# Four graph layers on one core: the heads' second scores go to every row by way of DRAM, and every kind of operation gets its own shift in the order

## The chip, the core and the metric

The kernel runs on one core of one Trainium2 chip. A core has five engines that each work through their own list of instructions: TensorE (matrix products; the profile calls it PE, and its weight loads PEld), VectorE (DVE), ScalarE (ACT), GpSimd (POOL) and SyncE (SP), which here only issues DMAs. An engine takes its instructions strictly in the order of its list, so an instruction that waits holds up all that stand behind it. The metric is the time of one execution on the device in microseconds (us); smaller is better.

## The reference, cut to what matters

The input `x` holds 128 graphs of 64 nodes with 512 features, in float32. All graphs share one 64 x 64 adjacency `adj`. Four layers follow each other, each `x = layernorm(x + layer(x))`. The first multiplies by `W` and aggregates over `adj`. The second is a graph attention with 4 heads, an output attention and a feed-forward part. The third and fourth are single-head attentions. The change lies in the attention of the four heads:

```python
Wh = jnp.einsum('bnf,hfo->bhno', x, W)
f1 = jnp.einsum('bhno,ho->bhn', Wh, a[:, :O])
f2 = jnp.einsum('bhno,ho->bhn', Wh, a[:, O:])
e = f1[:, :, :, None] + f2[:, :, None, :]
e = jnp.where(e > 0, e, LEAKY_ALPHA * e)
e = jnp.where(adj[None, None] > 0, e, NEG_INF)
attn = jax.nn.softmax(e, axis=-1)
```

For every head and graph, `e[n, m]` is a first score of node n plus a second score of node m. On the chip node n is a row (a partition), so the second scores, which lie one to a row, have to be brought into every row, along the free dimension. How they get there is what changes.

## The kernel before

The 8192 rows of `x` (128 graphs x 64 nodes) are cut into 32 pairs (`p`) of two tiles (`t`) of 128 rows. One tile holds two graphs. A pair goes through stages, each a Python generator: `stage_first` (layer one), `stage_scores` (scores and attention weights of the four heads, and the aggregated rows `ys`), `stage_heads` (the products of the heads with `W_heads`), `stage_project` (the product with `W_out`), `stage_out` (output attention, feed-forward part, norms), and `stage_gat` twice (layers three and four). The last pair has its own stages for the tail. The large products are done with seven half-size products in place of eight (`seven`, `strassen`), and the right-hand parts for them stream in from DRAM all the time (`ws_...`, from copies `d_...` that the kernel wrote there at its start). About five pairs are under way at once, each in another stage.

Nothing is issued while the stages run. `Plan.note` records each operation as a `Step` with a rank (its number, minus 1000 inside `nc.soon()`). Then `Plan.order` goes through all steps as a list scheduler would. It keeps a clock for each of the five engines, takes durations from the table `cost`, adds `WAIT` plus a `SLACK` between engines, hands out the buffers of the pools (`NEAR` says how far ahead of its turn a step may take one), and whenever an engine is free it takes the ready step of the lowest rank. `Plan.play` issues the steps in the order that comes out. All instructions are therefore issued from one line, L314, and the profile tells them apart only by the names of their tiles.

The heads' attention of a pair is `attention_heads`. `f` is a 128 x 2 x 8 tile: for each row the first and the second score of 4 heads in 2 tiles (8 columns each). For pairs 0 and 1 `f` comes from products on PE (`fp`), for the other 30 from dot products on VectorE (`dots`, tiles `j`), against score rows that are broadcast from DRAM (`rows<-d_h`). The spreading of the second scores before the change:

- VectorE multiplies the 8 second scores with `ident2`, two 64 x 64 identities on top of each other, into `dg`, 128 x 512 (8 blocks of 64 columns, each a diagonal);
- PE multiplies `dg` with `bones`, a 128 x 128 matrix with two 64 x 64 blocks of ones, into the PSUM tile `bc`: row n of `bc` then holds the second scores of all 64 nodes of its own graph, for 8 heads and tiles;
- VectorE adds the first score to it (`e`), and goes on with leaky relu, mask, maximum, subtraction, ScalarE's exp, sum, reciprocal and a last product, back into `e`;
- PE transposes `e` (`pt`), ScalarE copies the result to `aT`, and PE multiplies it with `x` (`yp`), the input of `stage_heads`.

The other attentions of the kernel spread their scores with transposes of a broadcast column (`attention`; also called `bc`, with `ident` and `f` as inputs) and are not changed.

Of the kernel before, what the change touches and what calls it, by code (L numbers as in the profile page):

```python
# [12 lines left out]
FP = mybir.dt.float32  # L13
# [3 lines left out]
ALU = mybir.AluOpType  # L17
# [3 lines left out]
P = 128  # L21
# [4 lines left out]
ts = lambda i, n: slice(i * n, (i + 1) * n)  # L26
# [11 lines left out]

WAIT = 0.2
NEAR = 160
SLACK = {"tensor": 0.8, "sync": 0.4}


class Slots:


    def __init__(self, n):
        self.free, self.queue = [(0.0, i, None) for i in range(n)], []  # L50
        self.openers = []
# [26 lines left out]
class View:  # L78
# [63 lines left out]
class Step:  # L142
    def __init__(self, engine, rank):
        self.engine, self.rank = engine, rank
        self.calls, self.after, self.behind, self.port = [], set(), set(), False
        self.opens, self.uses = [], set()
        self.takes, self.lands = 0.0, 0.0


class Plan:  # L150
# [23 lines left out]
    def note(self, engine, name, args, kw):  # L174
        if self.joined:
            s = self.joined[0]
            assert s.engine == engine
        else:
            s = Step(engine, len(self.steps) - self.early)
            self.steps.append(s)  # L180
            if self.joined is not None:
                self.joined.append(s)
        out = [kw[k] for k in ("out", "accum_out") if k in kw] + (
            [] if "out" in kw or not args else [args[0]]
        )
        views = [(v, True) for v in out if isinstance(v, View)] + [
            (v, False)
            for v in [*args, *kw.values()]
            if isinstance(v, View) and not any(v is o for o in out)
        ]  # L190
        for v, writes in views:
            t = v.tile
            writes = writes or t.pool.space is PSUM
            if not t.seen:
                s.opens.append(t)
            else:
                s.behind.add(t.seen[0][0])
            s.uses.add(t)
            s.after.update(o for o, r, w in t.seen if (w or writes) and v.meets(r))
            t.seen.append((s, v.region, writes))  # L200
        s.after.discard(s)
        s.behind -= {s} | s.after
        s.calls.append((name, args, kw))
        takes, s.lands = cost(engine, name, args, kw, out)
        if engine in ("vector", "gpsimd"):

            both = [v for v, writes in views if not writes and v.tile.pool.space is not PSUM]
            s.port = len(both) > 1 and (engine == "vector" or size_of(out) > 2)
        s.takes += takes

    def order(self):
# [21 lines left out]
        def late(s, e):  # L233
            return 0.0 if s.engine == e else WAIT + SLACK.get(s.engine, 0.3)

# [3 lines left out]
        def take(slots):  # L239

            while slots.queue:
                s = slots.queue[0][1]
                while slots in slots.openers[-1].given:
                    slots.openers.pop()
                if s.no > slots.openers[-1].no + NEAR:
                    return
# [62 lines left out]
    def play(self):  # L309
        real = lambda v: v.real() if isinstance(v, View) else v  # L310
        with self.tc.manual_schedule():
            for s in self.order():
                for name, args, kw in s.calls:
                    getattr(getattr(self.tc.nc, s.engine), name)(  # L314
                        *map(real, args), **{k: real(v) for k, v in kw.items()}
                    )
# [35 lines left out]
def gnn_stack_kernel(  # L352
# [24 lines left out]
    nc = Plan(tc)  # L377
    NT, D = x.shape
    N = adj.shape[0]
# [3 lines left out]
    G = T * H  # L383
# [56 lines left out]
    ident2 = cp.tile([P, N], FP, tag="ident2", name="ident2")  # L440
# [5 lines left out]
    never = cp.tile([P, 1], FP, tag="never", name="never")  # L446
# [12 lines left out]
    has = cp.tile([P, 1], FP, tag="has", name="has")  # L459
# [19 lines left out]
    aTg = [cp.tile([P, T, P], FP, tag=f"aTg{i}", name=f"aTg{i}") for i in range(2)]  # L479
# [44 lines left out]
    for h in range(H):  # L524
        w = wp.tile([P, KC // 2, 7, D // 2], FP, tag=f"wh{h}", name=f"wh{h}")
        for s in range(2):
            nc.sync.dma_start(
                out=w[:, :, 2 * s : 2 * s + 2, :].rearrange("p c h o -> p c (h o)"),
                in_=W_heads[h, ts(s, D // 2), :].rearrange("(c p) o -> p c o", p=P),
# [199 lines left out]
                    accum_out=f(s, t),  # L729
                )  # L730

    def attention_heads(f, name):

        bc3 = [P, G, N]

        dg = unit.tile([P, G, N], FP, tag="dg", name=f"dg_{name}")
        nc.vector.tensor_tensor(
            dg,
            f[:, 1, :].unsqueeze(2).to_broadcast(bc3),
            ident2.unsqueeze(1).to_broadcast(bc3),  # L740
            ALU.mult,
        )
        yield 2.0
        ps = psum.tile([P, G, N], FP, tag="b", name=f"bc_{name}")
        nc.tensor.matmul(ps, lhsT=bones, rhs=dg, start=True, stop=True)

        e = unit.tile([P, G, N], FP, tag="e", name=f"e_{name}")
        nc.vector.tensor_tensor(e, ps, f[:, 0, :].unsqueeze(2).to_broadcast(bc3), ALU.add)
        nc.vector.scalar_tensor_tensor(ps, e, 0.01, e, ALU.mult, ALU.max)
        nc.vector.copy_predicated(  # L750
            ps, mask1.unsqueeze(1).to_broadcast(bc3), fill1.unsqueeze(1).to_broadcast(bc3)
        )
        mx = small.tile([P, G], FP, tag="mx", name=f"mx_{name}")
        nc.vector.tensor_reduce(mx, ps, AX.X, ALU.max)
        nc.vector.tensor_tensor(ps, ps, mx.unsqueeze(2).to_broadcast(bc3), ALU.subtract)
        nc.scalar.activation(ps, ps, AF.Exp)
        sm = small.tile([P, G], FP, tag="sm", name=f"sm_{name}")
        nc.vector.tensor_reduce(sm, ps, AX.X, ALU.add)
        r = small.tile([P, G], FP, tag="r", name=f"r_{name}")
        nc.vector.reciprocal(r, sm)  # L760
        nc.vector.tensor_tensor(e, ps, r.unsqueeze(2).to_broadcast(bc3), ALU.mult)
        yield 10.0

        pt = psum.tile([P, G // 2, P], FP, tag="b", name=f"pt_{name}")
        with nc.together():
            for q in range(G // 2):
                nc.tensor.transpose(
                    pt[:, q, :], e[:, 2 * q : 2 * q + 2, :].rearrange("p s j -> p (s j)"), ident
                )
        aT = unit.tile([P, G // 2, 2, N], FP, tag="aTh", name=f"aT_{name}")  # L770
        for b in range(2):
            for s in range(2):
                nc.scalar.copy(aT[ts(b, N), :, s, :], pt[ts(s, N), :, ts(b, N)])
        return aT
# [64 lines left out]
    ys = {}  # L839
# [54 lines left out]
    def stage_scores(p):  # L894
# [4 lines left out]
        f = small.tile([P, 2, G], FP, tag="f", name=f"f_{p}")  # L899
        if p < 2:  # L900

            ps = psum.tile([P, T, 2, H], FP, tag="b", name=f"fp_{p}")
            for t in range(T):
# [14 lines left out]
        for h2 in range(H // 2 if p >= 2 else 0):  # L918
            for s in range(2):
                r = rows([score["h"][s * H + 2 * h2 + i, :] for i in range(2)], f"{p}_{h2}_{s}")  # L920
# [3 lines left out]
                    x, r, f"1_{p}_{h2}_{s}",  # L924
                )
        yield 3.0
        aT = yield from attention_heads(f, f"1_{p}")
        yield 3.0


        yh = []
        for q in range(H // 2):
            y = unit.tile([P, KC, 2, T, P], FP, tag="ys", bufs=2, name=f"ys_{p}_{q}")
            for t in range(T):
                ps = [
                    psum.tile([P, KC, 2, N], FP, tag="b", name=f"yp_{p}_{q}_{t}_{b}")
                    for b in range(2)
                ]
# [411 lines left out]
```

## Time and profile before

| what | value |
|---|---|
| median of three timed runs | 3346.63 us (3344.84 to 3348.06) |
| the profiled execution: its time, and its span from the first to the last instruction | 3347.62 us, 3345.8 us |
| PE, busy share of the span | 98% (3284.4 us) |
| PE weight loads | 86% |
| VectorE, ScalarE, GpSimd | 72%, 41%, 50% |
| DMA engines, mean busy share; moved | 64.9%; 718 MB |
| granted PE clock, mean | 0.993 |
| products `bc<-dg` (2 records each) | 64 records, 33.7 us busy |
| products `dg` on VectorE | 32, 22.5 us busy |

A PE record in this profile is longer than the spacing at which records follow each other, since they overlap in the pipeline; so what an operation costs on PE is read from the start of one group to the start of the next in the timeline. One float32 product shows as two records, a transpose as one.

### The profile page before, as it was taken

The page shows a single profiled execution, that of the slowest core. Times are in us where ns is not written, and L with a number is a line of the kernel's source. Part 1 is how long each engine was busy: PE and PEld are TensorE (multiplying, and loading weights), DVE is VectorE, ACT ScalarE, POOL GpSimd, SP SyncE. Part 2 cuts the span into 40 slices and gives each one's busy share as a digit, 9 for nine tenths or more (in the row PEclk, how much of TensorE's full clock was granted, in tenths as well). Part 3 has the DMA queues.
Part 4 walks back from the last instruction along what each step waited for, and adds up shares of the span by engine and source line. Part 5 has one row for each costly group of instructions (what it writes and reads, how often), then busy time and mean ns, then how long its engine had stood idle before and what let it go on. Part 6 is the DMA issues. An engine that isn't in the chain of part 4 may idle for free.

```text
span 3345.8 us, 59820 instructions
## 1 busy us (share of the span) xinstructions
PE 3284.4 (98%) x21298; PEld 2888.7 (86%) x21298; DVE 2420.4 (72%) x5698; ACT 1363.8 (41%) x3196; POOL 1684.7 (50%) x1860
## 2 busy tenths in 40 slices
PE   8999999999999999999999999999999999999997
PEld 4888888988988988989888989889889889888884
DVE  5477677777777777777777777777777777777756
ACT  2444344444444443443443443434444444444332
POOL 6745345554455554455554555544555544555442
PEclk9999999999999999999999999999999999999998
DMA  8956656667666666666666666676666666666752
GB/s 309 323 168 199 216 197 215 214 212 235 203 216 218 215 215 224 200 224 215 217 226 213 200 224 218 210 232 204 209 220 216 217 228 201 217 217 208 243 183 66
DMA packets 301062, 718.08 MB, mean 215 GB/s; under 512 B 32560, under 2 KB 41824, under 8 KB 300768
## 3 DMA queue, kind: packets, MB, share of 16 engines
q1 hardware_dynamic: 300768, 714.27, 64.9%
q8 instruction: 171, 2.80, 0.3%
q14 instruction: 123, 1.01, 0.1%
HBM read 680.82 MB, written 33.32 MB: 213 GB/s over the span
## 4 chain that ended last, share of the span: by engine, by line
PE 93%; DVE 2%; DMA 2%; POOL 2%; issue 1%; ACT 0%; SPq 0%; POOLq 0%; DVEq 0%
PE stx_h L314 13%; PE stx_o L314 13%; PE stx L314 12%; PE sty_h L314 10%; PE sty_o L314 10%; PE sty L314 9%; PE hidp L314 5%; PE yp L314 4%; PE gp L314 3%; PE stx_y L314 3%; PE sty_y L314 2%; PE axp L314 2%; PE bc L314 1%; DMA rows<-d_h 1%; PE op L314 1%; PE l L314 1%
## 5 line engine op out<-in xcount | busy, mean ns | idle before, releaser
L314 DVE CUSTOM_DVE_ANT_0 j<-x,rows 128x512 bf16<-128x512 f32 x736 | 627.9, 853 | 53.5 <-DMA rows<-d_h 23.0
L314 PEld LDWEIGHTS stx_h<-ys,wh 128*128 128x128 f32 x3072 | 392.0, 192 | 16.3 <-issue 0.9
L314 PE MATMUL stx_h<-ys,wh 128*128 128x128 f32 x3072 | 404.7, 275 | 1.1 <-DVE r_1o L314 0.8
L314 ACT COPY hT<-stx_h 128x256 f32<-128x256 f32 x384 | 142.9, 373 | 480.1 <-PE stx_h L314 335.8
L314 POOL TENSOR_SCALAR rs<-mv 128x1 f32<-128x1 f32 x256 | 70.8, 277 | 501.9 <-DVE mv L314 492.0
L314 ACT ACTIVATE x<-x,sh,rs 128x512 f32<-128x512 f32 x256 | 209.1, 817 | 203.8 <-DVE sh L314 202.9
L314 PE MATMUL sty_h<-ys,wh 128*128 128x128 f32 x2048 | 274.0, 277 | 2.8 <-ACT hT L314 2.8
L314 POOL TENSOR_TENSOR ys<-ys,t 128x256 f32<-128x256 f32 x128 | 114.5, 896 | 302.2 <-PE sty_h L314 302.0
L314 PEld LDWEIGHTS sty_h<-ys,wh 128*128 128x128 f32 x2048 | 249.6, 192 | 7.9 <-ACT hT L314 3.7
L314 PE MATMUL stx_o<-ws_wo_T,s_o 128*128 128x256 f32 x1024 | 246.1, 383 | 3.6 <-ACT who L314 2.7
L314 PE MATMUL sty_o<-ws_wo,hT 128*128 128x256 f32 x1024 | 242.4, 380 | 2.5 <-DMA ws_wo<-d_wo 2.5
L314 PE MATMUL hidp<-oT,w 128*128 128x256 f32 (+1 forms) x1056 | 231.1, 373 | 0.0
L314 DVE TENSOR_TENSOR hT<-sty_h,hT 128x256 f32<-128x256 f32 x256 | 107.9, 422 | 150.1 <-PE sty_h L314 146.8
L314 PEld LDWEIGHTS hidp<-oT,w 128*128 128x128 f32 x1056 | 193.5, 190 | 24.9 <-issue 0.5
L314 PEld LDWEIGHTS sty_o<-ws_wo,hT 128*128 128x128 f32 x1024 | 190.0, 190 | 27.1 <-DMA ws_wo<-d_wo 2.7
L314 DVE TENSOR_TENSOR x<-stx,x 128x256 f32<-128x256 f32 x360 | 149.2, 420 | 87.1 <-PE stx L314 83.6
L314 PEld LDWEIGHTS stx_o<-ws_wo_T,s_o 128*128 128x128 f32 x1024 | 186.0, 191 | 28.8 <-ACT who L314 3.6
L314 DVE SCALAR_TENSOR_TENSOR hT<-elu,hT 128x512 f32<-128x512 f32 x256 | 174.8, 684 | 40.6 <-ACT elu L314 37.1
L314 ACT ACTIVATE elu<-hT 128x512 f32<-128x512 f32 x256 | 153.7, 601 | 70.0 <-DVE hT L314 66.7
L314 DVE BATCH_NORM_STATS2 st<-x 128x6 f32<-128x512 f32 x256 | 177.0, 691 | 5.5
L314 ACT COPY ys<-yp 128x512 f32<-128x512 f32 x256 | 131.7, 600 | 114.1 <-PE yp L314 113.2
L314 DVE TENSOR_TENSOR x<-sty,x 128x512 f32<-128x512 f32 (+1 forms) x180 | 100.1, 556 | 87.2 <-PE sty L314 84.1
(201 smaller groups left out, 7719.3 us busy)
## 6 DMA issues: line engine op xcount, KB each, us to landing
ws_wo_T<-d_wo_T SPq DMA_DIRECT2D x256, 512.0 KB, 3.7
ws_wo<-d_wo SPq DMA_DIRECT2D x192, 512.0 KB, 3.9
ws_W_T<-d_W_T SPq DMA_DIRECT2D x248, 256.0 KB, 3.6
rows<-d_h SPq DMA_DIRECT2D x240, 256.0 KB, 4.7
ws_w_T<-d_w_T SPq DMA_DIRECT2D x112, 512.0 KB, 3.3
ws_W<-d_W SPq DMA_DIRECT2D x186, 256.0 KB, 3.7
ws_w<-d_w SPq DMA_DIRECT2D x84, 512.0 KB, 4.1
rows<-d SPq DMA_DIRECT2D x128, 256.0 KB, 4.8
```

Of the source, the lines that this page charges most:

```text
L314: getattr(getattr(self.tc.nc, s.engine), name)(*map(real, args), **{k: real(v) for k, v in kw.items()})
```

## The change

Two things change.

First, `attention_heads` gets a flag, true for pairs 0 and 1. For these nothing changes but a name (`dg` is now `over`). For the other 30 pairs the product with ones goes away. PE transposes the 8 second scores of all rows to an 8 x 128 PSUM tile (`f2p`), ScalarE copies it to SBUF (`f2`), SyncE stores it to a DRAM tile (`d_f`, 4 KB, as 2 graphs x 8 x 64), and two more DMAs broadcast each graph's 8 x 64 numbers to that graph's 64 rows of `over` (128 x 512 in SBUF). VectorE then adds the first score from `over` in place of `bc`. The PSUM tile `bc` stays as the place of the later steps. The generator yields 8.0 instead of 2.0 at this point.

Second, the order: `WAIT` goes from 0.2 to 0.152, `NEAR` from 160 to 150, and `Plan.play` adds to each step's rank a shift from the table `LATER`, chosen by the engine's first two letters and the name of the tile that it writes. A suffix `/S` or `/E` limits a shift to the first 11% or the last 7% of the steps. So the ordering of every engine's list changes from end to end.

```diff
-WAIT = 0.2
-NEAR = 160
+WAIT = 0.152
+NEAR = 150
+LATER = {
+    "gp:never/S": -100, "gp:rs_i": -60, "gp:s_o/S": -20, "gp:ys/E": -40, "sc:aT": -100,
+    "sc:aTg/S": 20, "sc:elu/S": -40, "sc:hT": 120, "sc:oT": 60, "sc:who": -80, "sc:xT": -200,
+    "sc:xT/S": -180, "sc:ys/S": 132, "sy:beta/S": -12, "sy:raw_w": 180, "te:fp/S": -20,
+    "te:hidp/E": -40, "te:hidp/S": 28, "te:l": 29, "te:l/S": 69, "te:pt": -28, "te:pt/E": 200,
+    "ve:e": -29, "ve:e/S": 40, "ve:f_o/S": -120, "ve:hT": 100, "ve:has": 200, "ve:mv": -100,
+    "ve:mv/E": 100, "ve:mx": -20, "ve:o": -140, "ve:r": -40, "ve:r/E": 40, "ve:sh": 10,
+    "ve:sm": -80, "ve:st": -13,
+}
...
+            n = len(self.steps)
+            for i, s in enumerate(self.steps):
+                when = "S" if i < 0.11 * n else "E" if i > 0.93 * n else "M"
+                s.rank += LATER.get(s.kind, 0) + LATER.get(f"{s.kind}/{when}", 0)
             for s in self.order():
...
-    def attention_heads(f, name):
+    def attention_heads(f, name, soon):
...
+        over = unit.tile([P, G, N], FP, tag="dg", name=f"over_{name}")
+        if soon:
...
+        else:
+            turned = psum.tile([G, P], FP, tag="b", name=f"f2p_{name}")
+            nc.tensor.transpose(turned, f[:, 1, :], ident)
+            f2 = unit.tile([G, P], FP, tag="e1", bufs=2, name=f"f2_{name}")
+            with nc.soon():
+                nc.scalar.copy(f2, turned)
+            d = dp.tile([2, G, N], FP, tag="d_f", bufs=2, name=f"d_f_{name}")
+            nc.sync.dma_start(
+                out=d.rearrange("b g j -> g b j"), in_=f2.rearrange("g (b j) -> g b j", b=2)
+            )
+            for b in range(2):
+                nc.sync.dma_start(
+                    out=over[ts(b, N), :, :], in_=d[b, :, :].partition_broadcast(N)
+                )
+            yield 8.0
+            ps = psum.tile([P, G, N], FP, tag="b", name=f"bc_{name}")
+        e = unit.tile([P, G, N], FP, tag="e", name=f"e_{name}")
         nc.vector.tensor_tensor(
...
+            e, ps if soon else over, f[:, 0, :].unsqueeze(2).to_broadcast(bc3), ALU.add
         )
...
-        aT = yield from attention_heads(f, f"1_{p}")
+        aT = yield from attention_heads(f, f"1_{p}", p < 2)
```

More of the change, by code (lines that the diff above doesn't have):

```diff
@@ L145, in __init__ @@
         self.calls, self.after, self.behind, self.port = [], set(), set(), False
+        self.kind = ""
         self.opens, self.uses = [], set()
@@ L203, in note @@
         s.calls.append((name, args, kw))
+        if not s.kind:
+            what = out[0].tile.args.get("name", "?") if out and isinstance(out[0], View) else "dram"
+            what = re.sub("__+", "_", re.sub(r"\d+", "", what).rstrip("_"))
+            s.kind = f"{engine[:2]}:{what}"
         takes, s.lands = cost(engine, name, args, kw, out)
@@ L730, in dots @@
                 )
-    def attention_heads(f, name):
+    def attention_heads(f, name, soon):
         bc3 = [P, G, N]
-        dg = unit.tile([P, G, N], FP, tag="dg", name=f"dg_{name}")
+        over = unit.tile([P, G, N], FP, tag="dg", name=f"over_{name}")
+        if soon:
+            nc.vector.tensor_tensor(
+                over,
+                f[:, 1, :].unsqueeze(2).to_broadcast(bc3),
+                ident2.unsqueeze(1).to_broadcast(bc3),
+                ALU.mult,
+            )
+            yield 2.0
+            ps = psum.tile([P, G, N], FP, tag="b", name=f"bc_{name}")
+            nc.tensor.matmul(ps, lhsT=bones, rhs=over, start=True, stop=True)
+        else:
[11 more added lines that the diff above has]
+                    out=over[ts(b, N), :, :], in_=d[b, :, :].partition_broadcast(N)
+                )
+            yield 8.0
+            ps = psum.tile([P, G, N], FP, tag="b", name=f"bc_{name}")
+        e = unit.tile([P, G, N], FP, tag="e", name=f"e_{name}")
         nc.vector.tensor_tensor(
[L738 to L741, printed above, removed]
-        )
[L743 to L748, printed above, removed]
+            e, ps if soon else over, f[:, 0, :].unsqueeze(2).to_broadcast(bc3), ALU.add
+        )
         nc.vector.scalar_tensor_tensor(ps, e, 0.01, e, ALU.mult, ALU.max)
```

## The prediction

> **What bounds the kernel now.** I read the first part of the page (busy shares), then PE's busy time by stretch, then the timeline where the change bites, then the waits and DMA issues.
>
> ```profile
> PE 3284.4 (98%) x21298; PEld 2888.7 (86%) x21298; DVE 2420.4 (72%) x5698; ACT 1363.8 (41%) x3196; POOL 1684.7 (50%) x1860
> ```
>
> PE and the others by stretch: each line has the stretch, its length, then busy time of PE, PEld, DVE, ACT, POOL, PE's granted clock, and the DMA engines' share and GB/s.
>
> ```profile
> 40.00:60.00 20.00, 19.82 (x93) 10.34 (x91) 14.84 (x35) 4.74 (x8) 15.42 (x16) 1.00 0.97 338
> 60.00:80.00 20.00, 18.07 (x54) 9.08 (x55) 9.38 (x14) 5.84 (x12) 19.52 (x17) 0.91 0.64 223
> 80.00:100.00 20.00, 12.80 (x97) 9.82 (x96) 14.61 (x21) 7.71 (x18) 10.36 (x8) 0.66 0.92 318
> ...
> 600.00:1000.00 400.00, 400.00 (x2644) 357.33 (x2643) 296.84 (x695) 166.96 (x390) 204.01 (x227) 1.00 0.66 217
> ```
>
> PE bounds the kernel: from 600 to 1000 us it is never idle. The span has 3345.8 - 3284.4 = 61 us of PE idle time. By stretches 24 us lie before 400 us (9 of them between 60 and 100, where the clock also falls to 0.91 and 0.66), 6 between 400 and 600, 3 from there to 3200, and 29 after it. A gain therefore has to come out of PE's work, or out of those idle places.
>
> In steady state, around 1600 us, the timeline (start, length, engine, group) gives PE's prices:
>
> ```profile
> 1613.64 0.27 PE L314 MATMUL pt<-ident,e 128*128 128x128 f32 x1
> 1613.75 1.06 PE L314 MATMUL stx_h<-t,wh 128*128 128x128 f32 x8
> ...
> 1626.88 1.02 PE L314 MATMUL bc<-dg,bones 128*128 128x512 f32 x2
> 1627.74 1.03 PE L314 MATMUL stx<-ws_W_T,s 128*128 128x256 f32 x4
> ```
>
> From start to start, a product with ones holds PE for 0.86 us, one transpose for 0.11 us.
>
> **What the Trainium skill says.** "Perfetto Trace Analysis", section "Identifying the Most-Contended Engine": matmul busy share overstates how full PE is, weight-load busy share is better. Here that is 86%, still the highest of all, and the starts show groups following without a gap, so I keep PE as the bound. "TensorE: Matmul & The Clock Gate", Part 1: the clock drops after an idle stretch of some 3.4 us and comes back only with sustained work. The trace agrees: 0.66 in the stretch with 7.2 us idle. "DMA: Bandwidth & Descriptors", "Anatomy of one DMA": about 2 us of a DMA is fixed, mostly the confirmation that the last byte has landed, and a wait is held by the issuing sequencer. The trace has these durations (below) and uses more.
>
> **The change, part by part.**
>
> *The product with ones, 30 pairs.* Removed: 30 x 0.86 = 25.8 us on PE. Added: 30 transposes `f2p` (8 columns of weights, 128 streamed). The nearest row is `wap`, 128 to 8, which takes 0.11 us in the stream like `pt`, so 30 x 0.11 = 3.3 us. Net -22.5 us, on the engine that bounds. Bounds -25.8 to -20.
>
> *VectorE.* `dg` goes: 32 take 22.5 us, so 21 us for 30. `e` stays and reads SBUF instead of PSUM; it had 689 ns, and `dg`, with two inputs in SBUF too, 704 ns. VectorE is at 72% and hides it. ScalarE gains 30 copies of 8 x 128, some 0.26 us each (`wat_h`, 32 x 128: 255 ns), 8 us at 41% busy, hidden.
>
> *DMA.* Three issues more per pair, 90 x about 0.4 us on SP's queue, 30 x (4 + 256) KB, 1% of 718 MB. Hidden, since the engines are 65% busy. What is not hidden for certain is the latency, since a transpose `pt` waits in PE's list for the end of the chain. From the end of `f2p`:
>
> ```profile
> ws_w<-d_w SPq DMA_DIRECT2D x93, 256.0 KB, 4.7
> rows_1o<-in_a_out_dram SPq DMA_DIRECT2D x64, 256.0 KB, 3.6
> rows_gamma<-in_gamma_dram SPq DMA_DIRECT2D x31, 256.0 KB, 4.8
> ...
> adj_i<-in_adj_dram SPq DMA_DIRECT2D x2, 16.0 KB, 2.0
> d_h<-wat_h SPq DMA_DIRECT2D x1, 16.0 KB, 4.0
> ```
>
> (The last number is us from issue to landing.) ScalarE sees PE's result 0.3 us after the transpose starts, copies in 0.26; the small store lands 2.0 to 4.0 us later, I take 3.0; the second of two loads is issued 0.4 later and lands after 3.6 to 4.8 us, I take 4.0. Sum 8.0 us, bounds 6.6 to 9.8. Then VectorE: from the start of `e` to the end of the last product into `e` the old kernel takes 1627.94 to 1636.13 = 8.2 us, with 13 steps of its list between them. In the changed list there are 16 in the tight pairs, three more at some 0.5 us: 9.7. Altogether 17.8 us. I counted the changed order of PE with the spacings of the timeline: between `f2p` and `pt` it puts 16.9 to 17.8 us of other work in 8 pairs (3, 5, 7, 9, 15, 17, 23, 25) and 18.7 to 26.7 in the other 22 (the old order: 9.8 from `bc` to `pt`). So 8 pairs are on the edge; late by 0.5 us each makes +4, with bounds 0 and 8 x 2 = 16.
>
> *SP's list.* The two loads wait for the store, and two to five weight loads stand between, so SP waits there 0.5 us or so at most in the middle case; behind them stand weight loads with 5.2 us or more of PE work before their use. One place is tighter by the new order alone: the first part of `w2` is asked for only 3.5 us of PE work before `sty_y` uses it, in 12 pairs, where the old order had 5.2 or more. Such loads landed in 3.1 to 4.7 us in the stretch I looked at; at 3.8 that is 0.25 us late, +3; bounds 0 and 12 x 1.2 = 14.
>
> *The order in the middle otherwise.* Counting steps of PE that wait for another engine with less than 1.8 us of PE work since that engine's own last input: 89 before, 80 after (700 to 2900 us). At 1.7 us the old trace has hardly a wait, so the new ones should not wait either, but for 9 places at 0.9 us, +1. The old kernel's own losses in the middle (PE's period is 101.2 us, but about 102 in 7 of 23 pairs, and 4.3 us once on `pt` waiting for `e`) I count as half gone, -5. Middle: 4 + 3 + 1 - 5 = +3.
>
> *The start.*
>
> ```profile
> 82.06 2.00 PE L314 MATMUL fp<-wa_h,x1T 128*128 128x8 f32 x16 [0.68 <-ACT x1T L314]
> 89.74 2.08 PE L314 MATMUL bc<-dg,bones 128*128 128x512 f32 x2 [5.68 <-DVE dg L314]
> 91.61 1.06 PE L314 MATMUL pt<-ident,e 128*128 128x128 f32 x4
> 93.50 6.12 PE L314 MATMUL yp<-aT,x 64*128 64x128 f32 x64 [0.84 <-ACT aT L314]
> ```
>
> Here PE has run out of layer-one products (`l`) and waits for pair 0's attention. `dg` of pair 1 stands on VectorE behind pair 0's chain, and that behind `sh`, which waits for GpSimd. In the changed order `fp` and `bc` of pair 0 stand before the second half of `l` of pair 2, and all of pair 3's `l` and both transposes lie between them and `yp`: some 16 us of PE work cover the same chain. Before, four steps between 60 and 100 us had no cover at all; after, none. At stake are 9.1 us of idle time and the slow clock's cost: `yp` x64 takes 6.1 us where 32 take 1.99 later, `l` x16 8.8 instead of 7.0, so 4 us more. I take -9; bounds -13 and 0, since new waits (ScalarE's copies of `ax` for pair 3 stand behind a norm that waits for GpSimd) may take 2 or more back. What is late next: GpSimd's halves for `W_out`, which have some 30 us.
>
> *The rest of the start and the tail.* From 130 to 700 us of PE work the old order has 17 steps with less than 1 us of such cover, the new one 14; in the last 140 us it is 23 and 29, in nearly the same sequence. 0, bounds -6 and +6.
>
> Sum: -22.5 + 3 - 9 + 0 = -28.5. The profiled execution took 3347.6 us (1.8 of it outside the span), so 3319.1; the median of the runs lies 1.0 lower: 3318 us, -0.85%.
>
> **The rivals.**
>
> *No new waits at all.* If store and load take 6.6 us and `w2` lands in time, the middle gives -5, the start -12, the tail -4: -43.5, so 3303. For it: VectorE gets 21 us back and the list is no tighter on the whole. Against it: SP's issues are busier.
>
> *The round trip partly late.* It takes 9.8 us, 1.8 longer: the 8 tight pairs lose 2 us each, 16; `w2` lands after 4.7 us, 14; nothing of the old losses goes. -22.5 + 30 - 9 = -1.5, or 3345; with half of these waits 3330. For it: landing times of 4.7 in the same stretch.
>
> *Slower.* One mechanism: SP stands still in front of the two loads until the store has landed. If the round trip is 12.5 us, the 8 tight pairs lose 4.7 us each (38) and the weight loads behind them come some 1 us late in all 30 (30): 68 - 31.5 = +36.5, or 3383. It decides from a round trip of about 10.5 us, where 30 pairs lose on average 1.05 us, the 31.5 us that products and start give. Against it: the broadcasts of the score rows, twice as large, never took over 7.1 us from issue to landing, and PE's cover in 22 pairs is larger.
>
> *The shifts undo the start.* If they bring no gain there (0 instead of -9): 3327.
>
> **How the numbers follow.** My own case (3318, itself 3308 to 3328, the undone start within it) has 0.58, no new waits 0.15, partly late 0.19 (of it 0.07 within 0.2% of no change, which is what a measurement here can tell: 3339.9 to 3353.3), slower 0.08. Range: from 3301 to 3343. Faster 0.85, same 0.07, slower 0.08.
>
> **What would show it.** Right: 30 `f2p` at 0.11 us and 4 records of `bc<-over`, PE busy lower by about 22 us, PE's period near 100.5 us between 600 and 3000 us; no wait over 2 us before 100 us, and `sty_h` starting at about 90 us instead of 99.6. Wrong: `pt` waiting for `e` or `e` for `over` in most pairs, SP waiting for `d_f` by more than 1 us each, `sty_y` waiting for `ws_w`, or periods of alternating length longer than 101.2 us.

## The result and the profile after

| | before | changed |
|---|---|---|
| timed runs side by side, median | 3347.35 us (3344.84 to 3350.77) | 3310.73 us (3310.24 to 3313.95) |
| ratio, 95% interval | 1 | 0.9892 [0.9875, 0.9909] |
| profiled execution; its span | 3347.62; 3345.8 us | 3313.95; 3312.2 us |
| PE busy; PE idle | 3284.4; 61.4 us | 3265.2; 47.0 us |
| VectorE busy | 2420.4 us | 2374.4 us |

The changed kernel is 1.1% faster: 36.6 us by the medians, 33.6 us by the two spans. The first part of the page, after:

```profile
PE 3265.2 (99%) x21268; PEld 2881.8 (87%) x21268; DVE 2374.4 (72%) x5668; ACT 1364.6 (41%) x3226; POOL 1724.0 (52%) x1860
```

In the views, `stx` and `sty` are the PSUM tiles of the half-size products: with `_h` those of `W_heads`, with `_o` those of `W_out` (VectorE adds them up in `who`), with `_y` those of the feed-forward part (added up in `o`), without a suffix those of the other layers. `ws_...` are their weights; a wait for one of these is a weight load that came late.

PE busy is 19.2 us lower, with 30 records fewer (two per product gone, one per transpose new), and PE's idle time 14.4 us lower. PE is still what bounds the kernel.

The stretches that the prediction shows of the kernel before, now in the changed kernel (PE, PEld, DVE, ACT, POOL, then PE's clock, DMA share, GB/s):

```profile
40.00:60.00 20.00, 19.69 (x79) 9.84 (x78) 15.00 (x42) 5.74 (x10) 14.94 (x15) 1.00 1.02 332
60.00:80.00 20.00, 18.02 (x61) 9.58 (x60) 12.13 (x17) 6.55 (x16) 19.44 (x16) 0.91 0.54 187
80.00:100.00 20.00, 19.93 (x165) 15.85 (x164) 10.01 (x15) 8.26 (x19) 14.55 (x12) 1.00 0.98 355
600.00:1000.00 400.00, 399.89 (x2653) 357.69 (x2652) 293.29 (x701) 168.65 (x399) 209.84 (x227) 1.00 0.68 220
```

From 80 to 100 us PE is now busy for 19.93 us at full clock, where it had been 12.80 us at 0.66. The timeline there shows the new order on PE:

```profile
65.23 1.02 PE L336 MATMUL bc<-over,bones 128*128 128x512 f32 x2
...
77.73 0.60 PE L336 MATMUL pt<-ident,e 128*128 128x128 f32 x4
...
83.38 2.95 PE L336 MATMUL yp<-aT,x 64*128 64x128 f32 x48
86.26 3.70 PE L336 MATMUL l<-w,ax 128*128 128x512 f32 x8
89.89 1.16 PE L336 MATMUL yp<-aT,x 64*128 64x128 f32 x16
90.98 1.12 PE L336 MATMUL bc<-over,bones 128*128 128x512 f32 x2
91.94 1.05 PE L336 MATMUL sty_h<-ys,wh 128*128 128x128 f32 x8
```

`bc` of pair 0 comes at 65 us, products `l` lie between it, `pt` and `yp`, and none of these lines carries a wait. `sty_h` starts at 91.94 instead of 99.55 us.

The spread itself, in one of the pairs where PE's work in between is shortest (timeline, 1501 to 1520 us):

```profile
1501.08 0.27 PE L336 MATMUL f2p<-ident,f 128*8 128x128 f32 x1
1501.19 1.03 PE L336 MATMUL sty<-ws_W,gT 128*128 128x256 f32 x4
1501.39 0.26 ACT L336 COPY f<-f2p 8x128 f32<-8x128 f32 x1 [1.52 <-PE f2p L336]
1501.67 0.29 SPq L336 DMA_DIRECT2D d_f<-f  x1
...
1504.40 1.09 SPq L336 DMA_DIRECT2D over<-d_f  x2
...
1508.78 0.69 DVE L336 TENSOR_TENSOR e<-over,f 128x512 f32<-128x512 f32 x1 [0.28 <-DMA over<-d_f]
...
1518.92 0.60 PE L336 MATMUL pt<-ident,e 128*128 128x128 f32 x4
```

The next product starts 0.11 us after `f2p`. The round trip to the start of `e` takes 7.7 us, and `pt` follows 17.8 us after `f2p` without a wait. What PE waits for from 100 to 3300 us, the first four lines of the list (total us, times, longest):

```profile
PE bc L336 <- DVE f L336: 6.0, 3, 3.5
PE gp L336 <- ACT aTg L336: 3.5, 5, 0.9
PE pt L336 <- DVE e L336: 3.0, 4, 1.1
PE stx_o L336 <- DVE who L336: 2.5, 1, 2.5
```

Of these only `pt` waiting for `e` can come from the new round trip. Two of its four waits, 1.9 us together, are those of the heads, at 419 and 512 us; the other two belong to the single-head attentions of the tail, which have an `e` and a `pt` too. In the kernel before the heads' `pt` waited once, for 4.3 us:

```profile
430.87 0.63 PE L314 MATMUL pt<-ident,e 128*128 128x128 f32 x4 [4.25 <-DVE e L314]
```

`e` waits for the loads 17 times on VectorE, but for 10.6 us in all, 1.6 at most.

To see where the time came from I cut each trace at the same three places: the first `sty_h` (pair 0), the `sty_h` group six pairs later, and that 24 pairs after it. All experiments are in the table too. The spans and stretches are those of single profiled executions: seven of the kernels have one and the same order up to the first `sty_h`, and take 89.4 to 91.9 us there, so a difference of some 2 us in one stretch shows nothing. The ratio, with its interval, comes from timed runs beside runs of the kernel before, and is what kernels are compared by across the table.

| kernel | to first `sty_h` | next 6 pairs | 24 pairs | rest | span | ratio [interval] |
|---|---|---|---|---|---|---|
| before | 99.6 | 638.4 | 2434.5 | 173.3 | 3345.8 | 1 |
| changed | 91.9 | 634.1 | 2419.7 | 166.5 | 3312.2 | 0.9892 [0.9875, 0.9909] |
| order_only | 90.7 | 629.8 | 2448.7 | 165.4 | 3334.6 | 0.9974 [0.9965, 0.9983] |
| dram_only | 100.7 | 641.4 | 2428.4 | 174.1 | 3344.6 | 1.0005 [0.9996, 1.0014] |
| product_back | 89.4 | 636.2 | 2438.5 | 165.4 | 3329.5 | 0.9963 [0.9948, 0.9978] |
| no_start | 100.3 | 635.7 | 2418.6 | 166.5 | 3321.1 | 0.9949 [0.9934, 0.9964] |
| no_tail | 90.6 | 634.8 | 2417.5 | 170.5 | 3313.4 | 0.9904 [0.9889, 0.9918] |
| no_all | 89.1 | 649.3 | 2432.2 | 174.5 | 3345.1 | 0.9993 [0.9986, 1.0000] |
| old_wait | 92.0 | 636.7 | 2451.6 | 171.9 | 3352.2 | 1.0061 [1.0044, 1.0078] |
| yield2 | 90.2 | 654.4 | 2499.6 | 173.6 | 3417.8 | 1.0226 [1.0210, 1.0241] |
| hop | 90.1 | 637.7 | 2457.8 | 164.7 | 3350.3 | 1.0038 [1.0023, 1.0053] |
| hop_late | 90.3 | 646.3 | 2456.4 | 165.6 | 3358.6 | 1.0038 [1.0023, 1.0053] |
| sp_stand | 89.4 | 638.4 | 2444.1 | 166.3 | 3338.2 | 0.9968 [0.9959, 0.9978] |
| over_later | 90.4 | 640.8 | 2449.6 | 164.8 | 3345.6 | 0.9989 [0.9981, 0.9998] |

Of the 33.6 us, 7.7 come before the first `sty_h`, 4.3 in the next six pairs, 14.8 in the 24 pairs of the middle, 6.8 after them. The 4.3 us may be the one wait at 431 us, of which 0.8 us are left at 419 in the changed kernel.

### The profile page after: what moved, and what is told of

It is laid out like the page before. It is cut to its first block, busy times and chain, and to the rows that moved or that the text cites. A ratio compares the mean times of both kernels' runs of the same rounds, so it can differ in the third digit from the quotient of the medians.

```text
span 3312.2 us, 60000 instructions
## 1 busy us (share of the span) xinstructions
PE 3265.2 (99%) x21268; PEld 2881.8 (87%) x21268; DVE 2374.4 (72%) x5668; ACT 1364.6 (41%) x3226; POOL 1724.0 (52%) x1860
## 4 chain that ended last, share of the span: by engine, by line
PE 91%; DVE 4%; DMA 3%; POOL 1%; issue 1%; ACT 0%; SPq 0%; POOLq 0%; DVEq 0%; ACTq 0%
PE stx_h L336 13%; PE stx_o L336 13%; PE stx L336 12%; PE sty_h L336 10%; PE sty_o L336 9%; PE sty L336 9%; PE hidp L336 7%; PE yp L336 4%; PE gp L336 3%; PE stx_y L336 3%; PE sty_y L336 2%; PE axp L336 2%; PE l L336 1%; PE op L336 1%; PE oTp L336 1%; DMA d_f<-f 1%
## 5 line engine op out<-in xcount | busy, mean ns | idle before, releaser
L336 DVE CUSTOM_DVE_ANT_0 j<-x,rows 128x512 bf16<-128x512 f32 x736 | 584.1, 794 | 94.3 <-DMA rows<-d_h 75.6
L336 PEld LDWEIGHTS stx_h<-ys,wh 128*128 128x128 f32 x3072 | 381.1, 192 | 22.3 <-DVE sh L336 5.7
L336 POOL TENSOR_SCALAR rs<-mv 128x1 f32<-128x1 f32 x256 | 104.1, 407 | 406.2 <-DVE mv L336 392.2
L336 POOL TENSOR_TENSOR ys<-ys,t 128x256 f32<-128x256 f32 x128 | 102.9, 814 | 189.8 <-PE sty_h L336 189.4
L336 POOL TENSOR_TENSOR rs<-rs,mhalf 128x1 f32<-128x1 f32 x256 | 173.4, 677 | 21.1
```

The costliest lines, as they stand in the source:

```text
L336: getattr(getattr(self.tc.nc, s.engine), name)(*map(real, args), **{k: real(v) for k, v in kw.items()})
```

## The experiments

My theory was that of the prediction: 30 products leave PE and give about 22 us, the order gives the start, and PE's other work hides the round trip. The rivals: the round trip is partly late, or SP's standing costs so much that the kernel gets slower.

**The two parts, each alone.** `order_only` keeps the product with ones in all pairs; `dram_only` has the spread by way of DRAM, no shifts and the old constants. In both the planner makes a new order from the steps that it is given, so neither has the order of the changed kernel or of the kernel before.

```diff
# order_only, from the changed kernel
-        aT = yield from attention_heads(f, f"1_{p}", p < 2)
+        aT = yield from attention_heads(f, f"1_{p}", True)
# dram_only, from the changed kernel
-WAIT = 0.152
-NEAR = 150
-LATER = {
...
-}
+WAIT = 0.2
+NEAR = 160
+LATER = {}
```

> The changed order for the kernel with the product with ones kept in all 32 pairs. Theory A (the two parts add up: 30 products cost 22.5 us on PE, the new order brings its share at the start and the end whatever the attention does): 3310.7 + 22.5 = 3333 us, or some 14 us less than before; sty_h of pair 0 starts near 92 us, PE busy is near 3285 us. In about 9 pairs this order leaves only 8.7 us of PE work between the product with ones and the transposes pt, where the chain in between takes 8.2 us, so some us on pt waiting for e may come on top: up to 3338. Theory B (the shifts only serve the DRAM spread): no gain by themselves, 3345 or more.

> The spread by way of DRAM with the old order's constants and no shifts. Theory A (parts add up): 3347.4 - 22.5 = 3325 us, with sty_h of pair 0 still near 99.6 us, since nothing at the start is moved; this order leaves 16.4 us of PE work between f2p and pt in three pairs and 19.9 or more in the others, against a chain of 16 to 18 us, so some 2 to 5 us may be lost on top: up to 3330. Theory B (the DRAM spread needs the new order): waits of pt for e in most pairs and 3340 us or more.

Measured: `order_only` 3335.48 us, 0.9974; `dram_only` 3346.38 us, 1.0005, no gain at all. Together they give 0.9892. So set one at a time the parts do not add up: alone they bring 0.3% and nothing, together 1.1%. (The time that theory A of `order_only` named, 3333 to 3338 us, did come out, but the kernel before took 3344 us beside it, so the gain is 9 us and not 14.) The table shows where. The order alone gains 8.9 us before the first `sty_h`, 8.6 in the next six pairs and 7.9 at the end, as the changed kernel does or better, but its middle is 14.2 us longer than before: PE idles there for 10.2 us in many short waits, against 2.8 in the kernel before, and is busy 6.8 us longer with as many records. The spread alone gains 6.1 us in the middle, and together it is 14.8. The products that PE no longer has are gone in `dram_only` as well (PE busy 3270.6 us, 13.8 less than before), but PE's idle time went from 61.4 to 74.0 us. Its waits in the middle, 700 to 3100 us, are on ScalarE's copies and small things, not on the spread:

```profile
PE sty L328 <- ACT gT L328: 5.0, 6, 0.8
PE stx_o L328 <- POOL s_o L328: 1.4, 3, 0.5
PE sty_y L328 <- DMA ws_w<-d_w: 0.6, 2, 0.3
```

These and the smaller ones add up to 8.8 us, against 2.8 in the kernel before and 3.7 in the changed one. `pt` does not wait for `e` there. Against the changed kernel the middle of `dram_only` is 8.7 us longer: PE has 5.7 us more idle time and 3.0 us more busy time there, the latter for a reason that the views do not show. Theory A falls for the middle and holds for the start; theory B of `dram_only` holds in its time, but not in its reason.

**The price of the product.** The order of every list stays as in the changed kernel; one product more stands in front of each `f2p`, so that PE does more work than the kernel needs.

```diff
# product_back, from the changed kernel
...
+            full = psum.tile([P, D], FP, tag="b", name=f"f2p_{name}")
+            turned = full[0:G, 0:P]
+            with nc.together():
+                nc.tensor.matmul(full, lhsT=bones, rhs=w1_sb[:, 0, :], start=True, stop=True)
                 nc.tensor.transpose(turned, f[:, 1, :], ident)
```

(The planner counts the additional product as zero, here and for the additional copies below, so that it makes the same order.)

> The changed kernel, every list in the same order, and in front of each of the 30 f2p one product with ones more, of a resident weight, whose result is overwritten: PE does more work than the kernel needs. Theory A (PE bounds, a product with ones costs 0.86 us in its list): +25.8 us, 3336.5. Theory B (PE has idle places that take it up, since f2p and all behind it are not urgent): +5 to +15 us. Theory C (it costs what its two records last, 0.59 us each): +35 us.

Measured: 3331.3 us, 0.9963, so 0.0071 of 3347 us or 24 us above the changed kernel by the ratios, 20.6 by the medians. In the 24 pairs of the middle it is 18.8 us, 0.78 us a product. In PE's list the product takes its 0.86 us:

```profile
1507.29 1.02 PE L338 MATMUL f2p<-w,bones 128*128 128x512 f32 x2
1508.15 0.27 PE L338 MATMUL f2p<-ident,f 128*8 128x128 f32 x1
1508.26 1.03 PE L338 MATMUL sty<-ws_W,gT 128*128 128x256 f32 x4
```

Theory A holds: PE bounds, and nine tenths of a product's spacing arrive in the time. With 0.11 for `f2p`, what the change takes from PE is worth 0.78 - 0.11 = 0.67 us a pair, 16.1 us in the 24 pairs. The changed kernel gains 14.8 of it, `dram_only` 6.1, so 10 less. (By the timed runs and all 30 pairs a product is worth 0.69 us, by the medians, to 0.79, by the ratios.)

This run also parts the gain with the order held, which the two runs above could not do. With the product put back, the changed order is still 0.37% faster than the kernel before (12 us): 10.2 us earlier at the first `sty_h` and 7.9 us shorter in the rest, but 4.0 us longer in the middle, though VectorE has no `dg` there. So about two thirds of the 36.6 us are the product. The other third is all else that changed, and it comes at the start and at the end.

**Which shifts.** Three kernels leave out one group of the table `LATER` each, a fourth keeps the table and puts the two constants back.

```diff
# each takes items out of LATER, or changes the constants
...
# no_start: without all items ending in /S      no_tail: without all items ending in /E
# no_all: only the items ending in /S or /E     old_wait:
-WAIT = 0.152
-NEAR = 150
+WAIT = 0.2
+NEAR = 160
```

> The changed kernel without the shifts of the first 11% of the steps (those ending in /S). Theory A (these shifts gave what was gained before 700 us: sty_h of pair 0 at 91.9 instead of 99.6 us, and some 4 us more up to 730 us): +8 to +12 us against the changed kernel, some 3321 us, with bc of pair 1 waiting for over again by 5 us or more. Theory B (the gain at the start comes from the unlimited shifts, from WAIT or NEAR): +3 us or less.

> The changed kernel without the shifts of the last 7% of the steps (those ending in /E). From the last sty_h group to the end the changed kernel takes 166.5 us, the kernel before 173.3. Theory A (the /E shifts give this): +7 us, 3318. Theory B (it comes from the unlimited shifts, or from the pair's position, as I had predicted nothing for the tail): 0 +-2 us.

> The changed kernel without the unlimited shifts (those without a suffix); WAIT 0.152, NEAR 150, /S and /E stay. With the DRAM spread alone the middle took 101.18 us a pair, in the changed kernel 100.82. Theory A (the unlimited shifts make this difference): +8 to +12 us in the middle, and some more where start and tail lean on them: 3319 to 3325. Theory B (WAIT and NEAR make it): +0 to +3 us.

> The changed kernel with all shifts, but WAIT 0.2 and NEAR 160 as before. Without the unlimited shifts the gain fell from 36 to 3 us. Theory A (shifts, WAIT and NEAR are one setting, each order that the planner makes from another one has its own waits): +10 to +30 us, spread over middle and start; this order has 21 places of PE with less than 1 us of work since the other engine's input could start, the changed one 9. Theory B (WAIT and NEAR do little): 0 to +5 us.

Measured: `no_start` 3327.68 us, with `sty_h` at 100.3 us and everything after it as in the changed kernel: in the profiled execution 8.9 us longer, 8.4 of them before the first `sty_h`. So these shifts make the start, theory A in its place, but not the 4 us of the next six pairs. Its timed runs lie between 3322.9 and 3332.5, the profiled one at the low end; what more the others lost no profile shows. `no_tail` 3313.14 us, its interval overlapping that of the changed kernel: the `/E` shifts bring nothing that the timed runs can tell (2.4 us by the medians). In its profiled execution the last stretch is 4.0 us longer. `no_all` 3341.86 us, 31 us above the changed kernel: nearly the whole gain goes with the unlimited shifts, 15 us in the six pairs, 12.5 in the middle and 8 at the end (the stretch to the first `sty_h` is as good as ever). `old_wait` 3364.06 us, slower than before by 0.6% and 53 us above the changed kernel; in its profiled execution, the fastest of its four, the middle is 32 us longer than in the changed kernel. In both, theory A was right and its size too small. The waits of `no_all` from 100 to 700 us begin with weight loads that come late:

```profile
PE sty L330 <- DMA ws_w_T<-d_w_T: 3.1, 1, 3.1
PE stx L330 <- DMA ws_w_T<-d_w_T: 2.9, 1, 2.9
PE yp L330 <- ACT aT L330: 2.8, 2, 2.5
```

Each of these is a single wait. No single shift was tried alone, so none can be named: each setting makes another order with other short waits, and table, constants and spread belong together.

**The yield.**

```diff
-            yield 8.0
+            yield 2.0
             ps = psum.tile([P, G, N], FP, tag="b", name=f"bc_{name}")
```

> The changed kernel with the generator's yield of 8.0 behind the loads put to 2.0, as it was before for the product with ones: the planner ranks e and what follows earlier. Between f2p and pt lie 13.8 us of PE work in three pairs and 17.3 in most others, where the chain takes 16 to 18 us. Theory A (the yield gives the cover that hides the round trip): pt waits for e by 2 to 3 us in three pairs and by some tenths in ten more, and 61 places of PE have under 1 us of cover (9 in the changed kernel): +15 to +35 us. Theory B (the planner knows the DMA's landing time anyway, and the yield matters little): 0 to +8 us.

Measured: 3420.18 us, 1.0226, 110 us above the changed kernel. Theory A was right on the side, and wrong on the size (15 to 35 us) and on the place: `pt` waits for `e` only 9 times, 6.3 us. The list from 300 to 3200 us is led by other steps:

```profile
PE stx_o L336 <- DVE who L336: 22.2, 28, 2.3
PE stx_y L336 <- DMA ws_w_T<-d_w_T: 15.2, 12, 1.8
PE stx_y L336 <- DVE o L336: 14.1, 11, 2.5
PE pt L336 <- DVE e L336: 6.3, 9, 1.4
```

What waits are half-size products that need VectorE's additions into `who` and `o`, that is, steps that stand on VectorE beside or behind those of the attention, and weight loads. But the yield also gave every engine another order, so this run can't tell one cause from another. The next four runs hold the order.

**A longer round trip, and SP standing.** In all four every list but SP's is in the order of the changed kernel. `hop` puts one more copy of the 4 KB, from DRAM to DRAM, behind the store; `hop_late` puts it in front of the two loads; `sp_stand` puts two of them behind the loads, the second waiting for the first, so that SP stands but `over` is not delayed; `over_later` copies nothing more and moves the two loads behind the next DMA of SP's list.

```diff
# hop (behind the store) and hop_late (in front of the loads)
...
+            nc.sync.dma_start(out=hop, in_=d)
...
-                    out=over[ts(b, N), :, :], in_=d[b, :, :].partition_broadcast(N)
+                    out=over[ts(b, N), :, :], in_=hop[b, :, :].partition_broadcast(N)
# sp_stand, behind the two loads
...
+                nc.sync.dma_start(out=hops[0], in_=d)
+                nc.sync.dma_start(out=hops[1], in_=hops[0])
# over_later, in play, for each step of the order from its end
...
+                if out[i].kind == "sy:over":
+                    j = i + 1
+                    while out[j].engine != "sync" or out[j].kind == "sy:over":
+                        j += 1
+                    out.insert(j, out.pop(i))
```

> The changed kernel, every list in the same order, with one more copy of the 4 KB from DRAM to DRAM between the store and the two loads: the round trip of f2p to the loaded rows gets one small DMA longer, some 2.5 us by the small stores of before (2.0 to 4.0), so about 10.5 us in the tight pairs. Theory A (PE's work covers the round trip, with about 1.7 us to spare in some 10 tight pairs and 2 to 3 us in the others): pt late by 0.8 us in the tight ones and by 0.4 in some more, +8 to +15 us. Theory B (SP stands still in front of the copy and again in front of the loads, and the weight loads behind come late): +30 us or more, with waits of stx and sty for ws tiles. Theory C (cover is ample, VectorE's steps behind e just follow closer): +0 to +3 us.

> The changed kernel, every list in the same order, with the additional copy of the 4 KB put directly in front of the two loads instead of directly behind the store. The round trip is longer by the same small DMA as in the run with the copy behind the store (+45 us), but the two to five weight loads that stand between store and loads are now asked for as early as in the changed kernel; those behind the loads come later. Theory A (the loss came from these weight loads, above all the first part of w2, with sty_y waiting 20 us for it): +5 to +20 us, sty_y hardly waits for ws_w. Theory B (the loss comes from the length of the round trip): +40 us or more again. Theory C (any stand of SP costs the same wherever it is): +40 us, with waits for the weight loads behind the two loads.

> The changed kernel, every list in the same order, with two more copies of 4 KB from DRAM to DRAM directly behind the two loads, the second waiting for the first: SP stands there for about 2 us (a small store was seen to land after 1.8 us) and issues two DMAs more (0.5 us each), but the rows in over come as early as in the changed kernel, which needs neither copy. With the additional copy between store and loads, SP stood 72 to 76 us in all and PE lost 38 us in the middle, 45 us in the median. Theory A (what costs is SP's standing, because weight loads behind it come late): +30 to +50 us again, with sty and stx waiting for ws tiles and e hardly for over. Theory B (what costs is that over and so the whole chain of VectorE is later): +0 to +10 us.

> The changed kernel with one move on SP's list: in all 30 pairs the two loads of over stand one DMA later, so that the store has more time to land and one weight load comes earlier. SP's waits for the store were 10 us in 9 pairs. Theory A (standing of SP costs PE about half its length, and PE's cover hides a later over): 0 to -5 us, 3306 to 3311. Theory B (the weight load that now stands ahead waits for PE to set its buffer free, so over comes some us later, and pairs with 1.7 us to spare make pt wait): +5 to +20 us.

| | changed | `hop` | `hop_late` | `sp_stand` | `over_later` |
|---|---|---|---|---|---|
| median of the timed runs, us | 3310.73 | 3356.17 | 3357.86 | 3334.99 | 3342.56 |
| SP waits for the store or the copy, us in all | 10 | 73 | 86 | 86 | 2 |
| `e` waits for `over` on VectorE, us (times) | 10.6 (17) | 39.9 (26) | 74.0 (30) | 1.5 (1) | 50.1 (27) |
| `f2p` to `e`, median us | 9.1 | 10.2 | 11.4 | 8.6 | 11.0 |
| the heads' `pt` waits for `e`, us (times) | 1.9 (2) | 1.4 (1) | 2.0 (2) | 0 | 2.8 (2) |

(SP's waits are those of 300 to 3200 us, those of `e` and `pt` of 100 to 3300 us, where the `pt` of the tail's other attentions are left out.) My theory A for `hop`, that PE's cover before `pt` sets what is lost, fell at once: +45 us instead of +8 to +15, and `pt` hardly waits in any of them. In `hop`, 300 to 3100 us:

```profile
PE sty_y L338 <- DMA ws_w<-d_w: 19.9, 16, 2.4
PE sty_y L338 <- DMA ws_w_T<-d_w_T: 6.0, 4, 2.3
PE stx_y L338 <- DVE o L338: 3.6, 5, 1.0
```

That is theory B, weight loads held behind a standing SP. `hop_late` was to spare these loads, and lost the same; what leads there is no longer `ws_w`, but 15.4 us on `ws_w_T` and 13.6 us on `o`. So two causes were mixed, and the last two runs have one each. `sp_stand` has the standing alone:

```profile
PE sty_y L339 <- DMA ws_w_T<-d_w_T: 17.4, 14, 2.1
PE sty_y L339 <- DMA ws_w<-d_w: 4.7, 5, 1.5
```

(100 to 3300 us.) It costs 24 us by the medians and 24.4 in the middle, with 76 us more of SP standing: about a third of it arrives on PE. Its theory A named this mechanism, with 30 to 50 us. `over_later` has the lateness alone: SP stands less for the store than in the changed kernel and PE waits for weight loads for only 3.0 us, and yet 32 us are lost (waits of 100 to 3300 us):

```profile
PE stx_y L343 <- DVE o L343: 25.5, 16, 3.6
PE pt L343 <- DVE e L343: 3.8, 4, 1.5
```

The weight load that was moved ahead waits for its buffer, `over` comes about 2 us later, and `e` stands on VectorE for it. Behind `e` in VectorE's list is the addition into `o` that PE's next product into the same PSUM tile waits for. The same place in both kernels, VectorE's and PE's timelines, first the changed kernel, then `over_later`:

```profile
1711.09 0.69 DVE L336 TENSOR_TENSOR e<-over,f 128x512 f32<-128x512 f32 x1 [0.91 <-DMA over<-d_f]
1711.82 1.11 DVE L336 SCALAR_TENSOR_TENSOR bc<-e 128x512 f32<-128x512 f32 x1
1712.84 0.41 DVE L336 TENSOR_TENSOR o<-stx_y,o 128x256 f32<-128x256 f32 x1
1713.31 1.13 PE L336 MATMUL stx_y<-ws_w_T,s_y 128*128 128x256 f32 x4
1714.28 1.89 PE L336 MATMUL stx_o<-ws_wo,hT 128*128 128x256 f32 x8
```

```profile
1726.89 1.71 DVE L343 TENSOR_TENSOR e<-over,f 128x512 f32<-128x512 f32 x1 [3.05 <-DMA over<-d_f]
1728.64 1.64 DVE L343 SCALAR_TENSOR_TENSOR bc<-e 128x512 f32<-128x512 f32 x1
1730.19 0.41 DVE L343 TENSOR_TENSOR o<-stx_y,o 128x256 f32<-128x256 f32 x1
1730.66 2.07 PE L343 MATMUL stx_y<-ws_w_T,s_y 128*128 128x256 f32 x4 [3.57 <-DVE o L343]
1732.53 3.62 PE L343 MATMUL stx_o<-ws_wo,hT 128*128 128x256 f32 x8
```

`e` waits 3.05 us instead of 0.91, and takes longer, and PE's `stx_y` stands 3.57 us for `o`, where it starts without a gap in the changed kernel. The stand costs more than its length: PE's granted clock is 0.50 from 1730.6 to 1736 us, and the products take 2.07 and 3.62 us instead of 1.13 and 1.89. In the middle of `over_later` PE's idle time is 20 us longer than in the changed kernel and its busy time 9.6 us, with three such stretches at half clock, where the changed kernel has none. Theory B of `over_later` was right that it loses, and wrong that it loses on `pt`. So in this order what is queued behind `e` on VectorE has less to spare than `pt` has: some 2 us of lateness use it up. None of these kernels is faster than the changed one.

## Why the prediction was right, point by point

The prediction was 3318 us, range 3301 to 3343; the changed kernel takes 3310.7.

- *The product with ones* (-22.5). 30 `f2p` at 0.11 us, as predicted. The product holds 0.86 us in PE's list but is worth 0.78 in time, so -20 instead of -22.5. PE busy fell by 19.2 us, not by 22. This term was a little too large.
- *VectorE and ScalarE hidden.* Right in this order: `e` takes 692 ns in the median, the copies 255 ns. `dg`'s time is gone. VectorE's busy time fell by 46 us and not by 21, the largest other part being the dot products `j`, at 794 ns in the mean instead of 853; that this was worth anything on PE no run shows.
- *The round trip* (8.0 us, 6.6 to 9.8). Measured in the eight tight pairs 7.7 to 8.3 us up to `e`, once 9.0. In the fastest the parts were 0.56 for transpose and copy, 2.8 from the copy's end to the first load's issue, 0.55 from there to the second, 3.8 until `e` starts: close to the 3.0, 0.4 and 4.0 of the prediction. VectorE's chain took 8.0 to 9.1 us there, once 10.3 (predicted 9.7), so `pt` had mostly 1.7 us to spare. The heads' `pt` waited for 1.9 us in all instead of 4, and only one of these two waits is in one of the eight pairs. The Trainium skill, "DMA: Bandwidth & Descriptors", "Anatomy of one DMA", has some 2 us fixed per DMA, but for DMAs that GpSimd issues. SP's are no such constant here: in `hop` the added copy lands after 1.8 us in the median, and the store lets SP go on 1.2 to 5.5 us after its issue.
- *SP's list and `w2`* (+3). `sty_y` waits for `ws_w` 1.3 us from 700 to 3100 us. SP waits for the store 9 times, 10.1 us in all, 1.4 at most, a little more than the 0.5 I allowed.
- *Middle otherwise.* I had +3 for all of the middle, so (24 pairs) about -16 net. Measured -14.8. The old losses are not simply halved: the 4.3 us on `pt` that I counted with them stand at 431 us, ahead of this stretch, and the period is no longer even but alternates between 92 to 94 and 107 to 110 us, 100.8 in the mean (100.5 predicted). I had named alternating periods longer than 101.2 us as a sign of being wrong; they alternate, two pairs at a time, but are shorter in the mean.
- *The start* (-9). `sty_h` at 91.9 instead of 99.6: -7.7; in nine of the ten experiments that keep the start's shifts it is at 89.1 to 90.7, so the predicted 90 is the usual value. No wait over 2 us stands there (the longest is 1.99, on `ax`, which I had named). `no_start` shows the cause.
- *Rest of start and tail* (0, -6 to +6). This term was mis-sized: the tail gave 6.8 us. It is lost again in `no_all` and `dram_only`, not in `order_only`, and by more than half in `no_tail` (170.5), so it needs the unlimited shifts and, by that one execution, the `/E` shifts too. In the tail of the kernel before `bc` waits once for 4.1 us for VectorE's `r` and `sty_o` for 2.5 us for a weight load; both waits stand in `dram_only` too (4.1 and 3.2) and neither in the changed kernel. Which shift removes them was not tried.

The sum holds in its mechanism, and its total is nearer than its terms: product and start gave less than predicted, the tail 6.8 us where I had put nothing. That these errors offset each other is luck. What failed was in the rivals. I counted the cover of the round trip on PE only, from `f2p` to `pt`, and asked of SP what stands behind its wait; I did not ask this of VectorE, where `e` waits. I had "slower" decide from a round trip of about 10.5 us in the tight pairs; in `over_later` (0.9989) the whole gain is gone at 9.7 us there (8.1 in the changed kernel), and for another reason than the one given. And the sum says nothing of how much the order must fit the steps: with the old constants and no shifts the same spread gains nothing.

## What to carry to other kernels

Work taken from the bounding engine becomes time only where the order around it fits; run each part alone before crediting one of them, and where a planner makes a new order for each part, also put the part back with the order held (`product_back`). Price a new latency by the list of the engine that waits for it, since what is queued behind the wait may be needed by the bounding engine sooner than the value waited for. To price one cost in a kernel with a planner, hold the order fixed and add the cost alone: two such runs (`sp_stand`, `over_later`) separated what two others had mixed.

## What the runs showed of the hardware

In the kernel before `e` read one tile in SBUF and one in PSUM; now it reads two in SBUF. In the changed kernel it still takes 692 ns in the median, and 4 of 30 take over 0.8 us; in `over_later` it is 14 of 30 and in `hop_late` 25 (median 1224 ns), the longest 1.8 us. In `yield2` it is 21, though `e` waits for its loads only 12 times there, so being late is not the cause by itself. In the place of `over_later` shown above GpSimd works at two-input additions all the while. The one beside `e` takes its usual 1.26 us, and `e` 1.71; in the same place of the changed kernel `e` takes its usual 0.69, and GpSimd's addition beside it 1.26 instead of 0.73. In both places the one that began later took longer. I had not counted with it, though the Trainium skill says so ("SBUF — State Buffer", "Who interferes with whom"): a VectorE instruction with two SBUF inputs contends with a GpSimd instruction that reads SBUF, and one of them blocks. The durations agree: over all 12 kernels with the spread, the 110 of 360 `e` that GpSimd's two-input instructions overlap by less than 30% of their length take 0.67 to 0.71 us, and all 108 that take over 0.8 us are overlapped by more. No run tested it by itself. The planner keeps such pairs of steps apart by its own clock (`port`), and a late `e` leaves the place that was kept for it; that lateness costs more than its own length for this reason is argued, not tested.

The prediction has the clock drop after some 3.4 us of idle time. Between 700 and 3100 us of `over_later` PE stands twice for 3.57 us and four times for 2.2 us. The half clock followed both long stands (at 1731 and 2344 us) and two of the short ones (at 709 and 1524 us), but not the other two (915 and 2550 us). So in this kernel a shorter stand can bring it, and not each does.
